# Message sums of a graph layer: half of the groups from rows split in two 12-bit parts, with a ring of 15 rows

## The chip, the cores and the metric

The kernel runs on one core of a Trainium2 chip. The metric is the device time of one execution in microseconds, the median of repeated runs. The engines are TensorE (PE, with its weight loads PEld), VectorE (DVE), ScalarE (ACT), GpSimd (POOL) and SyncE (SP). DMAs are issued from the queues of SyncE and ScalarE, and from POOL for gathers and scatters by index.

## The reference, cut to what matters

There are 6250 tokens of 256 values and 100000 edges sorted by target. The layer adds a graph convolution and a linear attention to its input, and then a mixture of 16 experts of which each token takes two.

```python
xn = _layernorm(x)
# graph convolution: the message sums are the second line
h = xn @ W
agg = segment_sum(norm[:, None] * h[src], dst)      # norm = dinv[src] * edge_weight * dinv[dst]
agg = agg + (dinv * dinv)[:, None] * h
# then + b, layer norm, mixing with xn, relu; attention over all tokens beside it
x = x + gcn + attention
# each token: two of 16 experts, (H=256 -> F=512 -> 256), weighted, layer norm
x = x + ffn(_layernorm(x))
```

## The kernel before, in words

The work of nearly every engine is put in order by hand. A loop counts slots; in each slot `c` from 0 to 781 POOL issues one gather of chunk `c` (128 edges), and all other steps are pieces that a `Weave` starts at given slots. An engine takes its instructions in the order in which they were emitted; POOL, SyncE and the others then run as fast as their waits allow.

Before the slots, the kernel turns the edges' targets, weights and sources into columns (`columns`: transposes on TensorE, copies on ScalarE), counts the degrees (`deg`), and writes the table `w_hs` to DRAM: the normalized rows of `x` times `dinv` (`table`, L522 and L524, staged in the big tile `Q`, stored by SyncE at L529).

In the slots, a chunk's message sum goes like this. At slot `c` POOL gathers 128 rows of 256 values from `w_hs` by the index column `src_t[:, c]` (L1306) into one of 12 rows of `rows3`, the ring `hrow`. VectorE builds a 128x128 matrix `hot` with the edge's weight where the target matches (L1310, a `tensor_scalar` of `iota_g` with two scalar columns). At slot `c + LAG`, LAG being 6, TensorE multiplies `hot` with the gathered rows in f32 (L1319; an f32 matmul is two instructions) into the group's accumulator. A group is 8 chunks. After its last chunk VectorE adds the accumulator, times `dinv`, into `agg` (L1331).

Woven in are: `attend` per token tile in the slots up to about 160 (keys, queries and the context; it writes its queries into `Q[:, t]` at L585), `own_term` (SyncE loads a tile of `w_hs`, ScalarE scales it, L648 and L650), the zero fills of `w_xslots` and `w_yslots` (L378, 1 MB each, on SyncE's queue), `residual` per pair of tiles from slot 171 on (transposes, products, layer norms: L688 to L756), `route` and `scatter` per phase of tiles (POOL writes tokens to slots of experts, L1005), `expert` per block of 128 slots (SyncE loads the weights, L1033; TensorE L1076, L1087 and L1098; ScalarE L1081 and L1094), and after the last chunk `combine` (POOL gathers the experts' rows, L1145). Memory that is free is handed on: `Places` gives tiles of `Q`, whose queries were read, to tokens, weights and results.

Of the kernel before, what the change touches and what calls it, by code (L numbers as in the profile page):

```python
# [22 lines left out]

F32 = mybir.dt.float32
BF = mybir.dt.bfloat16
I32 = mybir.dt.int32
# [86 lines left out]
NB3 = 2 * D  # L113
LAG = 6

# [17 lines left out]
def group_of(c):  # L133

    return (c + CPR // 2) // CPR


# [38 lines left out]
def gps_layer(ctx: ExitStack, tc: tile.TileContext, x, src, dst, ew, **rest):  # L176
# [6 lines left out]

    rows3 = top.tile([P, 3, EW], F32, name="rows3")
    loc_e, src_e, ew_e = rows3[:ER, 0, :], rows3[:ER, 1, :].bitcast(I32), rows3[:ER, 2, :]
    ident = top.tile([P, P], F32, name="ident")

    loc_t = top.tile([P, NCA], F32, name="loc_t")
    w_t = top.tile([P, NCA], F32, name="w_t")
    flag = top.tile([1, 1], I32, name="flag")  # L190
    with tc.tile_pool(name="chk", bufs=1) as cp, \
            tc.tile_pool(name="chk_ps", bufs=1, space=bass.MemoryType.PSUM) as cps, by_hand(tc):
        dst_e = cp.tile([ER, EW], I32, name="dst_e")
        v.memset(dst_e[:, PADC:], N - 1)
# [5 lines left out]
        for t0 in range(0, NFULL, 8):  # L200
# [25 lines left out]
        v.tensor_reduce(tot, n_out, axis=AX.X, op=OP.add)  # L226
        v.tensor_scalar(flag, tot, 0.0, None, op0=OP.is_equal)
    ok = nc.values_load(flag[0:1, 0:1], min_val=0, max_val=1,
                        skip_runtime_bounds_check_because="a comparison's result")
    with tc.If(ok) as cmp:  # L230
        windowed_layer(tc, X, rows3, ident, loc_t, w_t, **rest)
    with cmp.Else():
# [9 lines left out]
@with_exitstack  # L242
def windowed_layer(ctx: ExitStack, tc: tile.TileContext, X, rows3, ident, loc_t, w_t, W, b, gamma, beta, wqT, wkvT, wprojT, bproj,
                   gate_w, gate_b, experts, f_gamma, f_beta, out):
    nc = tc.nc
    v = nc.vector
    act = nc.scalar.activation
    src_e = rows3[:ER, 1, :].bitcast(I32)

# [6 lines left out]
    xslots = dram.tile([(MOST + 1) * P, D], F32, name="w_xslots")  # L256
    yslots = dram.tile([(MOST + 1) * P, D], F32, name="w_yslots")
    b2rows = dram.tile([NE * P, D], BF, name="w_b2rows")
    hand = ctx.enter_context(ExitStack())
    hand.enter_context(by_hand(tc))  # L260

    def one(shape, name, dt=F32):
        return keep.tile(shape, dt, name=name)


    iota_row = one([P, P], "iota_row")
    nc.gpsimd.iota(iota_row, pattern=[[1, P]], base=0, channel_multiplier=0,
                   allow_small_or_imprecise_dtypes=True)

    iota_g = one([P, 2, P], "iota_g")  # L270
    nc.gpsimd.iota(iota_g[:, 0, :], pattern=[[-P // 2, 2], [1, P // 2]], base=P // 2, channel_multiplier=0,
                   allow_small_or_imprecise_dtypes=True)
    nc.gpsimd.iota(iota_g[:, 1, :], pattern=[[1, P]], base=0, channel_multiplier=0,
                   allow_small_or_imprecise_dtypes=True)
# [27 lines left out]
    ones3 = one([3, P], "ones3", BF)  # L302
    src_t = one([P, NCA], "src_t", I32)

# [67 lines left out]

    def fill(a, first, end):

        zero = zero_b.bitcast(F32)
        for s in range(first, end, 8):
            q = min(8, end - s)
            nc.sync.dma_start(a[s * P:(s + q) * P, :].rearrange("(p q) c -> p q c", q=q),  # L378
                              zero[:, None, :].to_broadcast([P, q, D]))
            yield 8  # L380

    SOON = 88
    for _ in fill(xslots, 0, SOON):
        pass
    with tc.tile_pool(name="deg", bufs=1) as sp, \
# [59 lines left out]
        for n in (C // 2, C // 2, C, C, C):  # L445
            lo1 = sp.tile([P, 16, C], BF, name="lo1", bufs=2)
            for i in range(16):
                v.tensor_scalar(lo1[:, i, :n], lo_b[:, c0:c0 + n], float(i), None, op0=OP.is_equal)
            hw = sp.tile([P, HI, 3, C], BF, name="hw", bufs=2)
            for i in range(HI):  # L450
                for s in range(3):
                    v.scalar_tensor_tensor(hw[:, i, s, :n], hi_b[:, c0:c0 + n], float(i), w3[:, s, c0:c0 + n],
                                           op0=OP.is_equal, op1=OP.mult)
            for c in range(c0, min(c0 + n, NCH)):
                g0 = 4 * group_of(c)
                h0 = g0
                while h0 < g0 + HI:
                    i = h0 // HB
                    h1 = min(g0 + HI, (i + 1) * HB)
                    nc.tensor.matmul(deg[:, i, (h0 - i * HB) * 3:(h1 - i * HB) * 3], lo1[:, :, c - c0],  # L460
                                     hw[:, h0 - g0:h1 - g0, :, c - c0].rearrange("p h s -> p (h s)"),
                                     start=False, stop=False)
                    h0 = h1
            if c0 == 0:
                sf = sp.tile([ER, EW], F32, name="sf")
                nc.scalar.copy(sf, src_e)
                columns(nc, sps, ident, sf, src_t)
                two_sums()
            c0 += n
# [45 lines left out]

    Q = sums.tile([P, NT, D], F32, name="Q")
    TG = 7

    def table(t):
        r = rows(t)  # L520
        if t % 4 == 1:
            act(Q[:r, t, :], X[:r, t, :], AF.Identity, bias=nmr[:r, t:t + 1], scale=rsd[:r, t:t + 1])  # L522
        else:
            v.tensor_scalar(Q[:r, t, :], X[:r, t, :], mv1[:r, t, 0:1], rsd[:r, t:t + 1],  # L524
                            op0=OP.subtract, op1=OP.mult)
        if t % TG == TG - 1:
            t0 = t + 1 - TG
            n = min(NFULL, t0 + TG) - t0
            nc.sync.dma_start(hs[t0 * P:(t0 + n) * P, :].rearrange("(t p) c -> p t c", p=P), Q[:, t0:t0 + n, :])  # L529
            if n < TG:  # L530
                nc.sync.dma_start(hs[NFULL * P:, :], Q[:rows(NFULL), NFULL, :])

# [28 lines left out]
    def attend(t):  # L561
# [22 lines left out]
        v.scalar_tensor_tensor(kf[:r], e[:r, 0, :], 1.0, pos[:r, 0, :], op0=OP.min, op1=OP.add)  # L584
        v.scalar_tensor_tensor(Q[:r, t, :], e[:r, 1, :], 1.0, pos[:r, 1, :], op0=OP.min, op1=OP.add)  # L585
        yield 2
        if t == 0:
            kx.extend((bank("kx0"), bank("kx1")))
        for j in range(2):
            nc.tensor.matmul(kx[j][:, :D + 1], kf[:r, j * P:(j + 1) * P], xn[:r], start=(t == 0), stop=(t == NT - 1))  # L590

    def context():
# [47 lines left out]

    def queries(t0):

        return Q[:, t0:min(NT, t0 + 2), :]

    def own_term(t):

        r = rows(t)
        nc.sync.dma_start(agg(t)[:r], hs[t * P:t * P + r, :])  # L648
        yield 4
        nc.scalar.mul(agg(t)[:r], agg(t)[:r], dinv[:r, t:t + 1])  # L650
        begun.add(t)

    def residual(ts_):
# [30 lines left out]

        q = Q[:r0, t0:t1, :]
        q8 = q.rearrange("p t c -> p (t c)").rearrange("p (h d) -> p h d", d=HEAD)
# [518 lines left out]
    def spare(t, n=1):  # L1205
        return range(t, t + n), lambda: Q[:, t:t + n, :].rearrange("p t c -> p (t c)")

    hrow = rows3.rearrange("p a (i d) -> p (a i) d", d=D)
    NROW = 3 * EW // D
    homes = {"token": Places(*[spare(t) for t in range(4)]),  # L1210
# [6 lines left out]
                          spare(22, 6), spare(28, 6)),  # L1217
             "more": Places(*[((), lambda i=i: hrow[:, i, :]) for i in range(NROW)], *[spare(t) for t in range(9, 13)]),
             "got": Places(*[spare(t) for t in range(35, NT)])}

# [11 lines left out]
    for a, first in (yslots, 0), (xslots, SOON):  # L1232
        weave.add(fill_at, fill(a, first, MOST + 1))
        fill_at += 8 * ((MOST + 8 - first) // 8)
# [7 lines left out]
    for n, b in enumerate(PHASES):  # L1242
        flush = b == NT
        for t0 in range(a, b, 2):
            t1 = min(b, t0 + 2)
            at = max(at, min(NCH, 16 * t1 + 4) + LAG + 3)
            weave.add(at, residual(range(t0, t1)))
            last_at = at
            for t in range(t0, t1):
# [33 lines left out]
    weave.add(last_at + RES, load_last())  # L1283
    weave.add(last_at + RES + 22, shift(range(NT - NROW - 4, NT), last))
    at = last_at + RES
# [10 lines left out]
    weave.add(ready + 38, load_again())  # L1296
    hrows, hots, accs = {}, {}, {}
    done = []
    slot = -PRE
    while slot <= NCH + LAG or weave.steps:  # L1300
# [3 lines left out]
        if 0 <= c < NCH:  # L1304
            hrows[c] = hrow[:, c % NROW, :]
            nc.gpsimd.indirect_dma_start(  # L1306
                out=hrows[c], out_offset=None, in_=hs,
                in_offset=IndirectOffsetOnAxis(ap=src_t[:, c:c + 1], axis=0))
            hots[c] = mp.tile([P, P], F32, name="hot", bufs=LAG + 1)
            v.tensor_scalar(hots[c], iota_g[:, group_of(c) % 2, :], loc_t[:, c:c + 1], w_t[:, c:c + 1],  # L1310
                            op0=OP.is_equal, op1=OP.mult)
        c = slot - LAG
        if 0 <= c < NCH:
            g = group_of(c)
            begin = c == 0 or group_of(c - 1) != g
            end = c == NCH - 1 or group_of(c + 1) != g
            if begin:
                accs[g] = aps.tile([P, D], F32, name="acc")
            nc.tensor.matmul(accs[g], hots.pop(c), hrows.pop(c), start=begin, stop=end)  # L1319
            if end:  # L1320
# [12 lines left out]
        weave.run(slot)  # L1333
        slot += 1
    msg.close()
    hand.close()
# [521 lines left out]
```

## Time and profile before

| | |
|---|---|
| median of 15 runs | 1468.66 us (1463.33 to 1472.24) |
| profiled execution | 1466.18 us, span 1464.3 us |
| busy, PE / PEld / DVE / ACT / POOL | 1228.6 / 993.9 / 955.8 / 501.1 / 960.9 us |
| first gather to last gather (L1306) | 102.0 to 1205.2 us |
| granted TensorE clock, mean | 0.933 |

A group's line gives line, engine, operation, the tiles out<-in, the count, then the busy time and the mean of one in ns, then the idle time of the engine just before these instructions with what ended most of it. A wait's line gives the total in us, the times and the longest. In a table of stretches each engine has its busy time and its number of instructions in brackets. In a timeline the columns are start in us, duration in us, engine, line, operation, tiles, shapes, count, and in square brackets the engine's idle time before it. TensorE's busy time is modelled and overlaps weight loads, so a full TensorE is not one at its peak.

### The profile page before, as it was taken

To read this page: it belongs to the slowest core of one execution; us is meant where nothing else is said; L and a number is where in the kernel's file an instruction comes from. 1 tells how busy PE (TensorE), PEld (TensorE's weight loads), DVE (VectorE), ACT (ScalarE), POOL (GpSimd) and SP (SyncE) were. 2 spreads that over 40 slices of the span, in tenths; PEclk is the share of its full clock that TensorE was granted. 3 is DMA by queue.
4 is the path that set the end of the run, shared out by engine and by line. 5 is a ranking of instruction groups with operands and counts; after the bars stand their busy time and mean duration, and the time that the engine had idled before them with its cause. 6 is when DMAs were issued, how large, how long until landed. Compare 5 with 4: busy or idle time off the path is not lost. (4 is left out here: it accounts for less than half of the span.)

```text
span 1464.3 us, 24332 instructions
## 1 busy us (share of the span) xinstructions
PE 1228.6 (84%) x6923; PEld 993.9 (68%) x6923; DVE 955.8 (65%) x3302; ACT 501.1 (34%) x1354; POOL 960.9 (66%) x999
## 2 busy tenths in 40 slices
PE   4879999978777788989879799788988997968880
PEld 3836666656665677868768687677877886857660
DVE  7954454458887484756847568375684666568885
ACT  2764444422222122313223122232332333434451
POOL 1017777777767777777777777777777773167643
PEclk9999999999877899999999899998999998989995
DMA  8989933333335678768778687776768886989993
GB/s 260 314 293 374 381 108 102 106 103 115 102 105 165 222 237 279 263 231 269 273 233 290 202 270 264 264 269 226 263 219 278 293 292 220 310 293 387 379 316 96
DMA packets 176921, 353.83 MB, mean 242 GB/s; under 512 B 26769, under 2 KB 116020, under 8 KB 176770
## 3 DMA queue, kind: packets, MB, share of 16 engines
q1 hardware_dynamic: 128790, 223.10, 43.9%
q0 software_dynamic: 47712, 128.17, 27.5%
q8 instruction: 61, 1.00, 0.3%
q10 hardware_dynamic: 268, 0.82, 0.2%
q14 instruction: 90, 0.74, 0.2%
HBM read 277.60 MB, written 74.38 MB: 240 GB/s over the span
## 5 line engine op out<-in xcount | busy, mean ns | idle before, releaser
L1306 POOL DMA_INDIRECT rows<-w_hs,src_t x782 | 756.3, 967 | 327.2 <-issue 96.6
L1319 PE MATMUL acc<-rows,hot 128*128 128x256 f32 x1564 | 448.8, 403 | 90.9 <-DMA rows<-w_hs,src_t 76.8
L1310 DVE TENSOR_SCALAR hot<-iota_g,loc_t,w_t 128x128 f32<-128x128 f32 x782 | 270.9, 363 | 282.2 <-PE acc L1319 275.5
L1319 PEld LDWEIGHTS acc<-rows,hot 128*128 128x128 f32 x1564 | 279.9, 199 | 168.8 <-issue 73.0
L1005 POOL DMA_INDIRECT w_xslots<-Q,slot_i x98 | 99.1, 1011 | 78.2 <-ACT Q L1081 39.6
L1098 PE MATMUL yp<-early,hT 128*128 128x256 f32 x592 | 147.8, 395 | 1.2 <-ACT hT L1094 1.1
L1145 POOL DMA_INDIRECT Q<-w_yslots,slot_i x98 | 99.6, 1016 | 68.0 <-DVE xn L1161 22.2
L1087 PE MATMUL hp<-Q,early 128*128 128x128 f32 x992 | 127.7, 285 | 9.9 <-ACT Q L1081 9.9
L1087 PEld LDWEIGHTS hp<-Q,early 128*128 128x128 f32 x992 | 124.9, 200 | 14.7 <-ACT Q L1081 12.0
L1094 ACT ACTIVATE hT<-hp,early 128x128 f32<-128x128 f32 x296 | 84.3, 368 | 143.7 <-PE hp L1087 107.0
L1098 PEld LDWEIGHTS yp<-early,hT 128*128 128x128 f32 x592 | 116.5, 200 | 18.8 <-ACT hT L1094 2.4
L1081 ACT COPY Q<-xtp 128x256 f32<-128x256 f32 x114 | 42.2, 370 | 224.0 <-PE xtp L1076 221.9
L1087 PE MATMUL hp<-Q 128*128 128x128 f32 x832 | 106.8, 284 | 7.9 <-ACT Q L1081 7.9
L1087 PEld LDWEIGHTS hp<-Q 128*128 128x128 f32 x832 | 103.8, 199 | 12.5 <-ACT Q L1081 10.6
L576 PE MATMUL kq<-early,xnT 128*128 128x512 f32 (+1 forms) x196 | 95.8, 613 | 3.6 <-ACT xnT L572 3.6
L324 ACT ACTIVATE sd<-mv,eps_t 128x2 f32<-128x2 f32 (+2 forms) x76 | 22.6, 298 | 216.3 <-DVE mv L320 210.7
L1098 PE MATMUL yp<-Q,hT 128*128 128x256 f32 x320 | 78.2, 389 | 1.6 <-ACT hT L1094 1.5
L706 PE MATMUL hp<-w_sb,two_a 128*128 128x256 f32 (+1 forms) x196 | 58.2, 449 | 19.4 <-ACT two_a L678 19.4
L1098 PEld LDWEIGHTS yp<-Q,hT 128*128 128x128 f32 x320 | 60.1, 194 | 11.3 <-ACT hT L1094 3.9
L1331 DVE SCALAR_TENSOR_TENSOR agg<-acc,dinv,agg 64x256 f32<-64x256 f32 x135 | 64.9, 481 | 2.8
L706 PEld LDWEIGHTS hp<-w_sb,two_a 128*128 128x128 f32 (+1 forms) x196 | 42.6, 225 | 30.4 <-ACT two_a L678 21.9
L1108 DVE TENSOR_TENSOR Q<-yp,early 128x256 f32<-128x256 f32 x61 | 25.7, 422 | 55.8 <-PE yp L1098 55.7
(306 smaller groups left out, 1741.2 us busy)
## 6 DMA issues: line engine op xcount, KB each, us to landing
early<-in_experts SPq DMA_DIRECT2D x61, 642.0 KB
early<-in_experts SPq DMA_DIRECT2D x62, 512.0 KB
Q<-in_experts SPq DMA_DIRECT2D x52, 512.0 KB
Q<-in_experts SPq DMA_DIRECT2D x27, 642.0 KB
w_xslots<-zero_b SPq DMA_DIRECT2D x16, 1024.0 KB
w_yslots<-zero_b SPq DMA_DIRECT2D x16, 1024.0 KB
Q<-w_xslots SPq DMA_DIRECT2D x114, 128.0 KB
w_yslots<-Q SPq DMA_DIRECT2D x114, 128.0 KB
```

The lines of the kernel that those rows point to most:

```text
L576: nc.tensor.matmul(kq[:r], xnT[:, k, :r], wkq[:, k, :], start=(k == 0), stop=(k == 1))
L706: nc.tensor.matmul(hp[:r0, i, :], agT[:, k, i * P:i * P + r0], w_sb[:, k, :], start=(k == 0), stop=(k == 1))
L1005: i = nc.gpsimd.indirect_dma_start(out=xslots, out_offset=IndirectOffsetOnAxis(ap=slot_i[:r, t, k:k + 1], axis=0), in_=y[:r], in_offset=No ...
L1081: nc.scalar.copy(xT, tp[:, :2, :])
L1087: nc.tensor.matmul(hp[:, f, :], w1[:, c, f * P:(f + 1) * P], xT[:, c, :], start=(c == 0), stop=(c == 1))
L1094: act(hT[:, f, :], hp[:, f, :], AF.Relu, bias=b1[:, f:f + 1], scale=1.0)
L1098: nc.tensor.matmul(yp[:, :D], hT[:, f, :], w2[:, f, :], start=(f == 0), stop=(f == FJ - 1 and not as_row))
L1145: g = nc.gpsimd.indirect_dma_start(out=got[i, k]()[:r], out_offset=None, in_=yslots, in_offset=IndirectOffsetOnAxis(ap=slot_i[:r, t, k:k + ...
L1306: nc.gpsimd.indirect_dma_start(out=hrows[c], out_offset=None, in_=hs, in_offset=IndirectOffsetOnAxis(ap=src_t[:, c:c + 1], axis=0))
L1310: v.tensor_scalar(hots[c], iota_g[:, group_of(c) % 2, :], loc_t[:, c:c + 1], w_t[:, c:c + 1], op0=OP.is_equal, op1=OP.mult)
L1319: nc.tensor.matmul(accs[g], hots.pop(c), hrows.pop(c), start=begin, stop=end)
L1331: v.scalar_tensor_tensor(agg(t)[p0:p1], acc[p0:p1, :], dinv[p0:p1, t:t + 1], agg(t)[p0:p1], op0=OP.mult, op1=OP.add)
```

## The change

For the groups below 24, and from 40 on for those with an odd number, a chunk is summed in another way. `hot` is then a plain 0/1 matrix in the type float32r, built for two chunks at once by a `tensor_tensor` comparison of `iota_g` with `loc_t`. The gathered row is multiplied by the edge's weight and split into two parts: ScalarE writes `high`, the product in float32r, and VectorE writes `low`, the exact product minus `high`. TensorE multiplies `hot` with `high` and with `low`. The other groups are summed as before, their `hot` matrices allocated in pairs.

The gathered rows get a ring of 15, `high` and `low` rings of 5 each. To make room, `rows3` and the conversion of the sources into columns move to the first pool (before the check of the edges decides the branch), `Q` shrinks from 49 to 36 tiles, the tiles of `w_hs` from 35 on are staged in places 7 to 20, the queries of tiles from 36 on are stored to a new DRAM tensor `w_q` and loaded again 8 slots before their `residual`, and what lay in the ring's and `Q`'s last tiles late in the kernel (`more`, `got`) moves to a pool `late` that is opened after the ring is closed. The later zero fills go from SyncE's queue to ScalarE's. LAG becomes 7 (6 for chunks not in parts), and the residuals start one slot later with it.

```diff
-LAG = 6
+LAG = 7
+SPLIT = 3
+QT = 36
+RING_ROWS, RING_PARTS = 15, 5
+def in_parts(g):
+    return g < 24 or (g >= 40 and g % 2 == 1)
...
+        sf = cp.tile([ER, EW], F32, name="sf")
+        nc.scalar.copy(sf, src_e)
+        columns(nc, cps, ident, sf, src_t)
...
-    def fill(a, first, end):
+    def fill(eng, a, first, end):
...
-            nc.sync.dma_start(a[s * P:(s + q) * P, :].rearrange("(p q) c -> p q c", q=q),
+            eng.dma_start(a[s * P:(s + q) * P, :].rearrange("(p q) c -> p q c", q=q),
...
-    Q = sums.tile([P, NT, D], F32, name="Q")
+    Q = sums.tile([P, QT, D], F32, name="Q")
+    staged = [t if t < 5 * TG else t - 4 * TG for t in range(NT)]
...
+        if t >= QT:
+            nc.sync.dma_start(w_q[(t - QT) * P:(t - QT) * P + r, :], q[:r])
...
+    def load_queries(ts_):
+        for i, t in enumerate(ts_):
+            r = rows(t)
+            nc.sync.dma_start(queries(ts_[0])[:r, i, :], w_q[(t - QT) * P:(t - QT) * P + r, :])
...
-        weave.add(fill_at, fill(a, first, MOST + 1))
+        weave.add(fill_at, fill(nc.scalar, a, first, MOST + 1))
...
+            if t0 >= QT:
+                weave.add(at - 8, load_queries(range(t0, t1)))
...
-            hrows[c] = hrow[:, c % NROW, :]
+            hrows[c] = rp.tile([P, D], F32, name="hrow", bufs=RING_ROWS)
...
-            hots[c] = mp.tile([P, P], F32, name="hot", bufs=LAG + 1)
-            v.tensor_scalar(hots[c], iota_g[:, group_of(c) % 2, :], loc_t[:, c:c + 1], w_t[:, c:c + 1],
-                            op0=OP.is_equal, op1=OP.mult)
-        c = slot - LAG
-        if 0 <= c < NCH:
+        c = slot - 3
+        if 0 <= c < NCH and c % 2 == 0:
+            full = [P, 2, P]
+            g = group_of(c)
+            if in_parts(g):
+                hot = mp.tile(full, FR, name="hot", bufs=4)
+                v.tensor_tensor(hot, iota_g[:, g % 2:g % 2 + 1, :].to_broadcast(full),
+                                loc_t[:, c:c + 2, None].to_broadcast(full), op=OP.is_equal)
+            else:
+                hot = mp.tile(full, F32, name="hot", bufs=4)
+                for i in range(2):
+                    v.tensor_scalar(hot[:, i, :], iota_g[:, g % 2, :], loc_t[:, c + i:c + i + 1], w_t[:, c + i:c + i + 1],
+                                    op0=OP.is_equal, op1=OP.mult)
+            hots[c], hots[c + 1] = hot[:, 0, :], hot[:, 1, :]
+        c = slot - SPLIT
+        if 0 <= c < NCH and in_parts(group_of(c)):
+            highs[c] = rp.tile([P, D], FR, name="high", bufs=RING_PARTS)
+            act(highs[c], hrows[c], AF.Identity, scale=w_t[:, c:c + 1])
+        c = slot - SPLIT - 1
+        if 0 <= c < NCH and in_parts(group_of(c)):
+            lows[c] = rp.tile([P, D], FR, name="low", bufs=RING_PARTS)
+            v.scalar_tensor_tensor(lows[c], hrows.pop(c), w_t[:, c:c + 1], highs[c].bitcast(F32), op0=OP.mult, op1=OP.subtract)
+        for c, parts in ((slot - LAG, True), (slot - LAG + 1, False)):
+            if not (0 <= c < NCH and in_parts(group_of(c)) == parts):
+                continue
...
+            if parts:
+                nc.tensor.matmul(accs[g], hot, highs.pop(c), start=begin, stop=False)
+                nc.tensor.matmul(accs[g], hot, lows.pop(c), start=False, stop=end)
+            else:
+                nc.tensor.matmul(accs[g], hot, hrows.pop(c), start=begin, stop=end)
...
+        if slot == NCH + LAG + 1:
+            ringed.close()
```

## The prediction

> **What bounds the kernel now.** I read the page first. TensorE is its busiest engine, but the chain of waits holds only the last 9 us, so a bound has to be found stage by stage. Next came the table by stretches, on the message stage.
>
> ```profile
> core 0: us, PE busy (x) PEld busy (x) DVE busy (x) ACT busy (x) POOL busy (x), PEclk, DMA share, GB/s
> 180.00:240.00 60.00, 60.00 (x239) 42.18 (x238) 29.70 (x86) 28.42 (x59) 45.68 (x48) 1.00 0.40 120
> 360.00:420.00 60.00, 45.75 (x202) 35.76 (x200) 51.61 (x164) 14.34 (x31) 42.03 (x43) 0.84 0.34 98
> 1140.00:1200.00 60.00, 58.76 (x352) 51.90 (x352) 34.16 (x99) 18.77 (x55) 45.60 (x48) 1.00 0.88 300
> ```
>
> TensorE's load swings; POOL starts 48 DMAs in nearly every 60 us, one per 1.25 us. So I took POOL's own groups, cut to 102 to 1206 us:
>
> ```profile
> L1306 POOL DMA_INDIRECT rows<-w_hs,src_t x782 | 756.3, 967 | 327.2 <-issue 96.6 <-DMA w_yslots<-zero_b 83.7 <-PE acc L1319 59.7
> L1005 POOL DMA_INDIRECT w_xslots<-Q,slot_i x80 | 79.9, 999 | 24.4 <-issue 14.3 <-DMA w_xslots<-Q,slot_i 6.7 <-DMA rows<-w_hs,src_t 1.2
> ```
>
> Leave out the 83.7 us before the first gather: 756.3 + (327.2 - 83.7) + 79.9 + 24.4 = 1104.1 us, the whole 1104 us stage. Is any of that idle time a real wait?
>
> ```profile
> POOL rows L1306 <- issue: 96.6, 317, 0.3
> POOL rows L1306 <- PE acc L1319: 59.7, 179, 4.2
> L1306 POOL DMA_INDIRECT rows<-w_hs,src_t x782: 942/946/1525, 102.0 to 1205.2; - x196
> ```
>
> Where nothing releases a gather, the gap before it is 96.6/317 = 0.305 us, so that is POOL's own overhead. The 179 gaps put down to TensorE cost 59.7 - 179 x 0.305 = 5.1 us beyond it, those of L1087 another 0.5. So 5.6 us of the stage waits for anybody. **POOL's gathers bound 102 to 1206 us**, at 0.946 + 0.305 = 1.251 us each; TensorE only keeps up. The other thing to explain is the gathers' spread: median 946 ns, mean 967, longest 1525. The timeline shows what stands beside the long ones:
>
> ```profile
> 186.40 0.41 DVE L584 SCALAR_TENSOR_TENSOR row<-two_a,two_b 128x256 f32<-128x256 f32 x1
> 186.56 1.07 POOL L1306 DMA_INDIRECT rows<-w_hs,src_t  x1 [0.30 <-issue]
> 186.73 0.42 DVE L585 SCALAR_TENSOR_TENSOR Q<-two_a,two_b 128x256 f32<-128x256 f32 x1
> ...
> 315.03 1.50 POOL L1306 DMA_INDIRECT rows<-w_hs,src_t  x1 [0.30 <-PE acc L1319]
> 315.04 0.68 DVE L688 TENSOR_TENSOR qk<-Q,ksum 128x512 f32<-128x512 f32 x1
> ...
> 858.82 0.69 DVE L712 TENSOR_TENSOR h<-hp,bias_b 128x512 f32<-128x512 f32 x1 [1.38 <-PE hp L706]
> 858.92 0.95 POOL L1306 DMA_INDIRECT rows<-w_hs,src_t  x1 [0.30 <-PE hp L706]
> ```
>
> L584 and L688 read two SBUF tensors. A gather beginning under one ends 0.82 us after it: 186.81 to 187.63, 315.72 to 316.53. An undisturbed gather takes 0.946, so it is held if the operation still runs 0.126 us after its start. L585, begun 0.17 us after a start, lengthens nothing and is itself not slowed. L712, with one operand in PSUM, holds nothing.
>
> **The change, part by part.** Slots pace the program: one gather each, so POOL's cost counts in full and the others' only past 1.25 us a slot. Chunks in parts: groups below 24 hold chunks 0 to 187, odd groups 41 to 97 hold 29 x 8 = 232; together 420.
>
> *VectorE.* Removed: 420 one-hots at L1310 (363 ns, one tensor input). Added: per two chunks a comparison of shape 128x256, two SBUF inputs (nearest row L1130, 407 ns), and per chunk a `low` of 128x256, two SBUF inputs and a scalar column (L1161, 482 ns). In the 180 row VectorE carries 29.70/48 = 0.62 us a slot; it becomes 0.62 - 0.36 + 0.20 + 0.48 = 0.94. That fits in 1.25, so its time costs nothing; without that cover 0.32 x 420 = 134 us would be at stake.
>
> *What these inputs do to POOL.* This is the term that counts. An operation of length d beginning at random against a period of 1.25 us holds the next gather for (d - 0.126)^2 / (2 x 1.25) on average: `low` 0.356^2/2.5 = 0.051, comparison 0.281^2/2.5 = 0.032 per pair or 0.016 per chunk. L1310 held nothing (one input). Sum 0.067 x 420 = 28 us. Bounds: 0 if every `low` falls behind a gather's start; 0.356 x 420 = 150 us if each begins just before one. `low` follows `high`, which follows a landing, and landings and ScalarE's queue vary, so random phase is nearest; but a delayed gather moves away from the next `low`, so I take 22.
>
> The Trainium skill's page "SBUF — State Buffer", section "Who interferes with whom", states the contention between a two-SBUF-input VectorE instruction and a GpSimd instruction that reads SBUF, but as a lock for the whole instruction: whichever starts first blocks the other. By that rule a `low` begun under a gather would also wait for its end, 0.47 us on average in three quarters of the cases, VectorE would reach 1.3 us a slot in the first stretch, and some 10 us would be added. The L585 row above speaks against that half, and the sum leaves it out.
>
> *ScalarE.* Added: 420 `high` scalings, 128x256 with one scale column (L650, 509 ns; with two columns L566, 602), and the 23 later fills, which SyncE issues now (L378: 654 ns shortest, 2771 median). First 188 slots: 28.42/48 = 0.59, + 0.51, + 23 x 0.654/188 = 0.08, is 1.18 a slot; it fits by 0.07. Upper ends: 0.59 + 0.60 + 0.34 = 1.53. I take the lower end: the median fill was issued into saturated queues (in the table of stretches 120 to 180 us shows a DMA share of 1.06), while spread over 188 slots they bring 1 MB per 10 us. Queued behind a `high` that waits for its gather are the attend steps, for which TensorE waits, and on VectorE behind `low` the sums into `agg` and the attend steps again; in the later groups, at 18.77/48 + 0.25 = 0.65 a slot, nothing is tight.
>
> *TensorE.* Two f32 matmul instructions per chunk go, 403 ns each; two single ones of the new type come. No row has the type. Consecutive f32 instructions of 256 columns begin 0.217 us apart (four at L1319 in 1.03 us), 10 bf16 ones of 512 columns at L477 take 2.33 us, 0.105 per 256. So a chunk goes from 0.43 to between 0.21 and 4 x 0.217 = 0.87 us: from -0.22 to +0.44. I take -0.22, since operands cut to 12 bits are nearest to bf16. Off the path it is worth nothing: POOL waits 5.6 us for others.
>
> *Ring and lag.* 15 rows instead of 12, released by `low` four slots after the gather or by TensorE after six: the 5.6 us of waits go, I take -4. Residuals begin one slot later, so does the end: +1.3. The rings of 5 parts let `high` run one slot behind TensorE: nothing while both have room.
>
> *Queues and start.* The fills leave SyncE; the 13 query stores and 13 loads join it. A load waits for a residual two pairs earlier, 32 slots back, and expert loads queue behind it: nothing. The staged tiles that are written twice wait for a store that was issued some 8 us earlier (L529's seven stores begin over 13.7 us): nothing. The table's last stores no longer share queues with two fills (-2 at best), while the moved conversion of `src` (L466 1.0, L153 1.6 us) may hold up the weights' region (+3 at worst): 0. The `late` rows are needed after 1206 us: 0.
>
> **Sum.** +22 - 4 + 1.3 = +19.3 us, none of it in the tail after 1206 us, whose engines carry the same work. The profiled execution took 1466.2 us (span 1464.3): 1485.5. The median of the runs shown, 1468.66, lies 2.5 above that one: 1488.
>
> **Rivals.**
> *Parts cost nothing and the ring's waits go* (faster): by the packets of the gathers' queue between 220 and 400 us a gather has landed 2.4 us after its start; `high` 0.5 and two hand-overs of some 0.2 let `low` run from 3.3 to 3.78, before the third next gather reads at 3.75 + 0.13. If ScalarE is always prompt, no gather is held: -5.6 - 2 + 1.3 gives 1462. It decides if `low` is late by less than 0.1 us; attend steps of 0.6 us in ScalarE's queue speak against it. Halfway (4 us of holding) nothing moves: 1468.
> *ScalarE becomes the bound in the first 188 slots*: with fills at the median 1.44 us a slot, with both upper ends 1.53: 188 x 0.19 to 0.28 = 36 to 53, and 16 of holding in the later 232 chunks: 1517 to 1536.
> *The new type doesn't run in one pass*: TensorE, full in the 180 row at 1.25 a slot, gets 0.44 more: 188 x 0.44 = 83 us, later covered in part: 1550 or more. The Trainium skill's "FP8 and Floating Point Precision", section "TensorE Precision Notes", counts four passes for true FP32 and tells of a reduced mode that reads 4 bytes and truncates; by it a chunk would take two passes instead of four, the lower end.
>
> **Chances.** Forecast 0.62 (lock 10 to 35 us: 1476 to 1502); faster 0.12; nothing moves 0.07; ScalarE 0.13; TensorE 0.06. A measurement here tells 0.2%, 2.9 us, from no change. Faster 0.12, same 0.07, slower 0.81. The range takes in the forecast, no change and most of ScalarE's case: 1465 to 1520.
>
> **What would show it.** Right: the gathers' mean rises from 967 to about 995 ns (22 us over 782) with the minimum at 942, and to about 1020 where all chunks are in parts, while groups 24 to 39 stay; gaps stay 0.305; TensorE's busy time falls. Wrong: the mean stays near 967 (the faster rival); POOL's gaps grow behind ScalarE or `high` (second) or behind matmuls (third); or the time after the last gather moves by more than 2 us, of which nothing here speaks.

## The result and the profile after

The changed kernel takes 1509.0 us (median of 9 runs, 1504.85 to 1516.7) against 1467.8 us of the kernel before beside it (46 runs): a ratio of 1.0279, 95% interval 1.0262 to 1.0297, 41 us slower. The profiled execution took 1502.9 us (span 1501.2), some 6 us below its median; against the profiled 1466.2 us of before that is 36.8 us, and this is what the traces can account for. The forecast was 1488, a change of 20 us: the sign and the main mechanism were right, the size was half of what came.

The table by stretches first (same columns as before).

```profile
core 0: us, PE busy (x) PEld busy (x) DVE busy (x) ACT busy (x) POOL busy (x), PEclk, DMA share, GB/s
180.00:240.00 60.00, 48.79 (x205) 32.08 (x203) 38.97 (x98) 40.59 (x94) 46.29 (x46) 0.94 0.60 188
360.00:420.00 60.00, 47.41 (x223) 36.42 (x221) 50.22 (x149) 17.43 (x39) 40.17 (x43) 0.89 0.35 102
```

In the first stretch TensorE's busy time went from 60 to 49 us, VectorE's rose from 30 to 39, ScalarE's from 28 to 41, all below 60; and POOL got 46 DMAs through instead of 48. So POOL still sets the pace, and it is slower. POOL's groups, cut to the gather stage (101 to 1243 us), then its waits there and the gathers' line:

```profile
L1338 POOL DMA_INDIRECT hrow<-w_hs,src_t x782 | 784.4, 1003 | 333.1 <-issue 97.1 <-DMA hT<-w_hs 84.2 <-PE acc L1376 24.9
L1025 POOL DMA_INDIRECT w_xslots<-Q,slot_i x80 | 82.0, 1025 | 24.4 <-issue 15.2 <-DMA w_xslots<-Q,slot_i 6.7 <-DVE mv L329 1.2
```
```profile
POOL hrow L1338 <- issue: 97.1, 314, 1.7
POOL hrow L1338 <- PE acc L1376: 24.9, 52, 3.8
```
```profile
L1338 POOL DMA_INDIRECT hrow<-w_hs,src_t x782: 942/946/2673, 103.7 to 1242.4; - x196
```

The 782 gathers are busy 784.4 us instead of 756.3 (mean 1003 ns instead of 967) with the same minimum and median; the longest now takes 2673 ns. The free gap stayed at 97.1/314 = 0.309 us (0.305 without the one of 1.7). From TensorE there are fewer waits, but 24.9 - 52 x 0.305 = 9.0 us of them lie beyond the free gap (5.1 before). The first gather starts at 103.7 instead of 102.0. The account of the two profiled executions:

| term | before | after | difference |
|---|---|---|---|
| first gather starts | 102.0 | 103.7 | +1.7 |
| gathers busy | 756.3 | 784.4 | +28.1 |
| scatters busy (80 in the stage) | 79.9 | 82.0 | +2.1 |
| all POOL gaps beyond 0.305 us | 5.4 | 10.6 | +5.2 |
| from the last gather's start to the end | 259.1 | 258.7 | -0.4 |

The sum, 36.7, is the whole difference. Now the gathers alone (line L1338), cut at chunks 188 and 316; the chunks between them are groups 24 to 39, of which none is in parts:

```profile
103.55:352.62 249.07, 191.77 (x188) 0.92 0.63 198
352.62:557.91 205.29, 124.86 (x128) 0.85 0.50 159
557.91:1243.55 685.64, 467.76 (x466) 0.93 0.75 252
```

191.77/188 is 1020 ns a gather where all chunks are in parts (975 before), 124.86/128 is 975 where none is (982 before), 467.76/466 is 1004 after that (960 before). And in that last stretch it is not the odd groups' own gathers that grew (964 to 971 ns by their records) but those of the even groups, 956 to 1036: in these groups most `low`s (155 of 232) start when POOL is five or more gathers further on, and 150 when it is at a later group.

What holds them is seen in the timeline:

```profile
182.98 0.41 DVE L1347 TENSOR_TENSOR hot<-iota_g,loc_t 128x256 fp32r<-128x256 f32 x1
183.31 0.86 DVE L1362 SCALAR_TENSOR_TENSOR low<-hrow,w_t,high 128x256 fp32r<-128x256 f32 x2
183.45 1.89 POOL L1338 DMA_INDIRECT hrow<-w_hs,src_t  x1 [0.30 <-DVE hot L1347]
184.11 0.41 DVE L1347 TENSOR_TENSOR hot<-iota_g,loc_t 128x256 fp32r<-128x256 f32 x1
...
610.46 1.72 POOL L1338 DMA_INDIRECT hrow<-w_hs,src_t  x1 [0.30 <-issue]
610.69 0.67 DVE L751 SCALAR_TENSOR_TENSOR X<-h,X 128x512 f32<-128x512 f32 x1
```

The gather that starts at 183.45, under the first of two `low`s, isn't released between them, nor between them and the comparison that follows without a pause: it ends at 185.34, 0.82 us after that comparison's end (184.52). That is not the rule, though. Another such pair, with a gather that starts as far into it (0.14 us), lets the gather go 0.82 us after the first one's end:

```profile
634.37 0.87 DVE L1362 SCALAR_TENSOR_TENSOR low<-hrow,w_t,high 128x256 fp32r<-128x256 f32 x2
634.51 1.16 POOL L1338 DMA_INDIRECT hrow<-w_hs,src_t  x1 [0.30 <-PE yp L1118]
```

Of 135 gathers held by an operation that another one followed without a pause, 116 ended 0.82 us after the first operation's end and 19 later; what decides between the two isn't known.

Now each gather's and scatter's time beyond its undisturbed one (946 and 973 ns) is put to the VectorE operation that runs some 0.06 us after its start. The total of 48.8 us (18.6 before) contains 20.9 of `low` (94 of the 152 that met one were over 30 ns longer), 7.0 of the comparisons (29 of 46) and 4.6 of six gathers like the one at 610.46, where L751 stands directly behind a sum into `agg`. Cut in another way, 36.3 us (13.4 before) lie up to 0.82 us after the end of the operation that was running when the gather started (0.85 for scatters; this takes in all that is lengthened by 30 ns or less), and 12.5 us (5.3 before) beyond that, under operations that began after the gather.

### The profile page after: what moved, and what is told of

Its sections match the earlier page's. It is cut to its first block, busy times and chain, and to the rows that moved or that the text cites. A ratio compares the mean times of both kernels' runs of the same rounds, so it can differ in the third digit from the quotient of the medians.

```text
span 1501.2 us, 25295 instructions
## 1 busy us (share of the span) xinstructions
PE 1204.4 (80%) x6923; PEld 974.7 (65%) x6923; DVE 1061.5 (71%) x3512; ACT 670.2 (45%) x1774; POOL 990.9 (66%) x998
## 5 line engine op out<-in xcount | busy, mean ns | idle before, releaser
L1338 POOL DMA_INDIRECT hrow<-w_hs,src_t x782 | 784.4, 1003 | 333.1 <-issue 97.1
L1362 DVE SCALAR_TENSOR_TENSOR low<-hrow,w_t,high 128x256 fp32r<-128x256 f32 x420 | 199.1, 479 | 138.3 <-ACT high L1358 133.1
L1358 ACT ACTIVATE high<-hrow,w_t 128x256 fp32r<-128x256 f32 x420 | 203.7, 506 | 208.3 <-DMA hrow<-w_hs,src_t 142.3
L1376 PE MATMUL acc<-hrow,hot 128*128 128x256 f32 x724 | 214.0, 410 | 37.6 <-DMA hrow<-w_hs,src_t 24.2
L1376 PEld LDWEIGHTS acc<-hrow,hot 128*128 128x128 f32 x724 | 128.6, 201 | 64.3 <-DVE hot L1352 21.0
L1373 PE MATMUL acc<-high,hot 128*128 128x256 f32 x420 | 159.8, 395 | 5.6 <-ACT high L1358 5.5
L1374 PE MATMUL acc<-low,hot 128*128 128x256 f32 x420 | 124.4, 309 | 35.3 <-DVE low L1362 33.9
L1165 POOL DMA_INDIRECT late<-w_yslots,slot_i x98 | 99.4, 1014 | 66.9 <-DVE xn L1181 20.9
L584 PE MATMUL kq<-early,xnT 128*128 128x512 f32 (+1 forms) x196 | 103.3, 652 | 39.5 <-ACT xnT L580 39.2
L1107 PEld LDWEIGHTS hp<-Q 128*128 128x128 f32 x832 | 104.4, 203 | 18.7 <-ACT Q L1101 17.9
L1352 DVE TENSOR_SCALAR hot<-iota_g,loc_t,w_t 128x128 f32<-128x128 f32 x362 | 108.3, 358 | 0.0
L1373 PEld LDWEIGHTS acc<-high,hot 128*128 128x128 f32 x420 | 86.4, 206 | 19.8 <-issue 10.9
```

The source lines that it names most:

```text
L584: nc.tensor.matmul(kq[:r], xnT[:, k, :r], wkq[:, k, :], start=(k == 0), stop=(k == 1))
L1107: nc.tensor.matmul(hp[:, f, :], w1[:, c, f * P:(f + 1) * P], xT[:, c, :], start=(c == 0), stop=(c == 1))
L1165: g = nc.gpsimd.indirect_dma_start(out=got[i, k]()[:r], out_offset=None, in_=yslots, in_offset=IndirectOffsetOnAxis(ap=slot_i[:r, t, k:k + ...
L1338: nc.gpsimd.indirect_dma_start(out=hrows[c], out_offset=None, in_=hs, in_offset=IndirectOffsetOnAxis(ap=src_t[:, c:c + 1], axis=0))
L1352: v.tensor_scalar(hot[:, i, :], iota_g[:, g % 2, :], loc_t[:, c + i:c + i + 1], w_t[:, c + i:c + i + 1], op0=OP.is_equal, op1=OP.mult)
L1358: act(highs[c], hrows[c], AF.Identity, scale=w_t[:, c:c + 1])
```

## The experiments

All kernels are variants of the changed one. "Waits" are POOL's gaps between the first and the last gather beyond 0.305 us each; "tail" runs from the last gather's start to the end; both, with the gathers and the first gather's start, are from each kernel's one profiled execution. The ratio is to the kernel before on the same chip, where its medians are 1467.8 to 1469.6 us.

| kernel | median us | ratio, 95% interval | first gather | gathers busy, mean ns | waits | tail |
|---|---|---|---|---|---|---|
| before | 1468.7 | | 102.0 | 756.3, 967 | 5.4 | 259.1 |
| changed | 1509.0 | 1.0279 [1.0262, 1.0297] | 103.7 | 784.4, 1003 | 10.6 | 258.7 |
| no_parts | 1478.6 | 1.0081 [1.0055, 1.0107] | 105.2 | 765.6, 979 | 4.1 | 259.8 |
| one_by_one | 1474.2 | 1.0052 [1.0033, 1.0072] | 106.3 | 762.3, 975 | 2.0 | 257.9 |
| extra_two | 1504.1 | 1.0252 [1.0217, 1.0287] | 106.9 | 781.7, 1000 | 5.2 | 262.1 |
| extra_one | 1490.7 | 1.0144 [1.0120, 1.0168] | 108.8 | 769.3, 984 | 4.8 | 261.4 |
| extra_psum_3 | 1485.4 | 1.0118 [1.0089, 1.0147] | 104.6 | 759.5, 971 | 10.0 | 263.7 |
| low_single | 1496.0 | 1.0199 [1.0166, 1.0233] | 105.2 | 769.6, 984 | 10.5 | 265.9 |
| hot_scalar | 1510.7 | 1.0284 [1.0253, 1.0315] | 104.4 | 783.0, 1001 | 12.9 | 262.8 |
| both_single | 1493.9 | 1.0179 [1.0155, 1.0203] | 106.8 | 763.8, 977 | 9.7 | 266.1 |
| until_20 | 1502.5 | 1.0237 [1.0214, 1.0261] | 105.3 | 778.8, 996 | 2.0 | 262.4 |
| late_only_3 | 1492.3 | 1.0182 [1.0145, 1.0218] | 105.0 | 769.7, 984 | 6.9 | 262.6 |

**What is left without the parts.** `no_parts`:

```diff
-    return g < 24 or (g >= 40 and g % 2 == 1)
+    return False
```

Expected: 

> No chunk goes in parts; the 15-row ring, the moved fills, the moved conversion of src, the smaller staging tile and the one-hots made in pairs all stay. Theory (two-input VectorE operations hold the gathers): the 30 us of holding and the 5 us of new waits in groups 24 to 39 go, the later start of 1.7 us may stay: 1467 to 1471, gather mean 967 ns. Rival (the ring, the moved queues or the paired one-hots cost the time): 1485 or more, with the gather mean at 967 all the same.

It came 8 to 12 us above the theory's 1467 to 1471 and below the rival's 1485. So the parts make some 30 of the 41 us, and something else costs 9. The gathers' mean is not 967 but 979, and the timeline shows an operation that the prediction had cleared:

```profile
137.80 0.59 DVE L1352 TENSOR_SCALAR hot<-iota_g,loc_t,w_t 128x128 f32<-128x128 f32 x2
138.13 2.01 POOL L1338 DMA_INDIRECT hrow<-w_hs,src_t  x1 [0.30 <-PE tp L552]
138.31 0.42 DVE L592 SCALAR_TENSOR_TENSOR row<-two_a,two_b 128x256 f32<-128x256 f32 x1
138.98 0.59 DVE L1352 TENSOR_SCALAR hot<-iota_g,loc_t,w_t 128x128 f32<-128x128 f32 x2
```

The one-hot has one tensor input, yet the gather that starts under a pair of them is held, through the attend steps and into the next pair: 9.2 us in all are held under L1352, where the kernel before had 2.0 under L1310. `one_by_one` makes them one a slot again:

```diff
-        if 0 <= c < NCH and c % 2 == 0:
-            ...
-                for i in range(2):
-                    v.tensor_scalar(hot[:, i, :], ...)
+        if 0 <= c < NCH:
+            v.tensor_scalar(hots[c], iota_g[:, group_of(c) % 2, :], loc_t[:, c:c + 1], w_t[:, c:c + 1],
+                            op0=OP.is_equal, op1=OP.mult)
```

Expected: 

> As no_parts (no chunk in parts), but each slot makes its own one-hot with one VectorE instruction, as the kernel before does, instead of two every second slot. Holding theory, with back-to-back runs as a part of it: the one-hots' holding (9.2 us in no_parts, 2.0 us in the kernel before) falls by 7 us, and about 3 us stay for the later first gather: 1470 to 1473, gather mean 979 falls to about 969 ns. Rival (the rest of the change, ring and queues, costs the 9 us): still 1477 to 1480.

1474.2, just above the theory's 1470 to 1473: 4.4 us go, not 7, and the intervals of the two ratios overlap (7.3 us are still held under the one-hots, which now run three slots later than in the kernel before). What stays above the kernel before, 0.5%, is in the profiled executions 6.0 us of gathers and 4.3 us of a later first gather, against 3.4 us fewer waits, with the ring of 15 rows.

**One operation alone.** On top of `one_by_one`, 420 VectorE operations were added that nobody reads, one for each chunk that the change takes in parts, and nothing on ScalarE or TensorE. The three differ in their operands:

```diff
+            extra = rp.tile([P, D], F32, name="extra", bufs=2)
+            v.scalar_tensor_tensor(extra, hrows[c], w_t[:, c:c + 1], hrows[c], op0=OP.mult, op1=OP.subtract)   # extra_two
+            v.tensor_scalar(extra, hrows[c], w_t[:, c:c + 1], w_t[:, c:c + 1], op0=OP.mult, op1=OP.subtract)   # extra_one
+            v.scalar_tensor_tensor(extra, hrows[c], w_t[:, c:c + 1], nothing, op0=OP.mult, op1=OP.subtract)    # extra_psum_3: nothing is in PSUM
```

Expected: 

> As one_by_one, plus one VectorE operation for each of the 420 chunks that the change would take in parts: row times weight minus row, 128x256, two SBUF inputs, into a tile that nobody reads; no high or low part, no new type, no work on ScalarE or TensorE. Holding theory: 13 us (each alone: a gather is held if it starts 0.08 to 0.36 us after the operation's start, so 0.28^2/2.5 = 0.030 us each) to 28 us (with its share in back-to-back runs), on top of one_by_one: 1484 to 1500. Rival (ScalarE's and TensorE's parts cost the time, not this operation): no more than 2 us on top of one_by_one.

Expected: 

> As extra_two, but the operation has one tensor input and the weight column twice: row times weight minus weight. Holding theory: the window is 0.15 to 0.28 us after its start, 0.13^2/2.5 = 0.007 us each, 3 us, up to 9 with runs: 3 to 9 us above one_by_one, and at least 10 under extra_two. Rival (VectorE's load or order delays others): within 3 us of extra_two, since the operation is nearly as long.

Expected: 

> As extra_two (one_by_one plus 420 operations of 128x256 that nobody reads), but the subtracted operand lies in PSUM, a tile of zeros, so that one tensor input is left in SBUF; the pool of the other PSUM tiles has 5 banks instead of 6 for it. Holding theory: an operation with a PSUM operand holds no gather by itself, so what is left is what it adds to runs: 1 to 6 us above one_by_one, 1.004 to 1.010 of the kernel before. Rival (the VectorE time of the operation or its wait for the row costs the 30 us of extra_two): 1.020 to 1.027.

`extra_two` costs 30 us over `one_by_one`, as much as the whole splitting in parts. That is 2 us past the end of its holding price, and 4 past the 1500 stated; in the profiled executions 19.4 us are gathers, 4.8 scatters. `extra_one` costs 16.5, more than the 3 to 9 expected, of which 7.0 are gathers, but it lies 13.5 under `extra_two`. With the operand in PSUM the gathers are as in `one_by_one` (759.5 and 762.3 us busy); the time is still 11 us above it, in waits (+8.0) and tail (+5.8). Its ratio of 1.0118 lies above the 1.004 to 1.010 expected and below the rival's 1.020. Whether the missing PSUM bank or VectorE's load makes these waits was not separated; `extra_two`, with the same load and all banks, has 5.2 us of them, but its gathers are held, which may give TensorE time. The same start of a gather, 0.19 us into the operation, first in `extra_two`, then in `extra_psum_3`:

```profile
158.52 0.48 DVE L1357 SCALAR_TENSOR_TENSOR extra<-hrow,w_t 128x256 f32<-128x256 f32 x1 [2.38 <-DMA hrow<-w_hs,src_t]
158.71 1.11 POOL L1338 DMA_INDIRECT hrow<-w_hs,src_t  x1 [0.30 <-DMA hrow<-w_hs,src_t]
```
```profile
151.86 0.47 DVE L1360 SCALAR_TENSOR_TENSOR extra<-hrow,w_t,nothing 128x256 f32<-128x256 f32 x1
152.05 0.94 POOL L1341 DMA_INDIRECT hrow<-w_hs,src_t  x1 [0.30 <-DVE hot L1347]
```

The first gather ends 0.82 us after the operation (159.00 to 159.82), the second takes its plain 0.94. Counted over all gathers that start 0.145 to 0.27 us after such an operation's start, and held by over 30 ns: 45 of 45 for `low` in the changed kernel, 42 of 42 in `extra_two`, 35 of 40 in `extra_one`, 4 of 56 in `extra_psum_3` (two for 37 and 38 ns, two for 0.7 and 0.8 us by operations with two SBUF inputs queued behind it). Under `low` the window opens some 0.08 us after the start (of 27 starts between 0.08 and 0.145, 26 were held), with one tensor and a scalar column at about 0.145; under the comparison L1347 it opens earlier (15 of 16 starts between 0.02 and 0.08 were held). So the mechanism is shown: at the same length on VectorE (medians 477 and 473 ns) and in the same order, the place of the operand decides whether a gather is held.

**The pieces of the changed kernel.** `low_single` and `hot_scalar` take the second SBUF tensor from one operation each, `both_single` from both. `low_single` and `both_single` leave out the true subtraction, so their sums differ.

```diff
-            v.scalar_tensor_tensor(lows[c], hrows.pop(c), w_t[:, c:c + 1], highs[c].bitcast(F32), op0=OP.mult, op1=OP.subtract)
+            v.tensor_scalar(lows[c], hrows.pop(c), w_t[:, c:c + 1], highs[c][:, 0:1].bitcast(F32), op0=OP.mult, op1=OP.subtract)   # low_single
-                v.tensor_tensor(hot, iota_g[:, g % 2:g % 2 + 1, :].to_broadcast(full), ...)
+                for i in range(2):                                                                                                # hot_scalar
+                    v.tensor_scalar(hot[:, i, :], iota_g[:, g % 2, :], loc_t[:, c + i:c + i + 1], None, op0=OP.is_equal)
```

Expected: 

> The low part is made from the row, its weight and one column of the high part as two scalars, so that it has one tensor input in SBUF instead of two but still waits for the high part; the true subtraction is left out. Holding theory: 20.9 us of holding by the low parts go: about 1488, gather mean 1003 falls to about 976 ns. Rival (the queueing behind ScalarE's high part, or TensorE's parts): the same order and the same waits, so no change, 1505 to 1510. Rival (VectorE's load): only what a shorter operation saves, under 8 us.

Expected: 

> The comparison of two chunks with two SBUF inputs (407 ns) is replaced by two comparisons with one tensor input and a scalar column each (some 360 ns each); nothing else changes. Holding theory: the 43 gathers that it held (7.0 us) are free, minus a little for a busier VectorE: 1500 to 1504. Rival (VectorE's load is what costs): 0.16 us more work for each of 420 chunks, 1515 or more. Gather mean in groups below 24: 1020 ns falls to about 1003 by the theory.

Expected: 

> Both edits: the low part with one tensor input (its true subtraction left out) and the comparisons with one tensor input each. Holding theory: 28 us go, 1479 to 1483, gather mean about 968 ns, and what is left above the kernel before is new waits in groups 16 to 39 and the later start. Rival (queueing or TensorE): 1505 or more, or slower for VectorE's longer comparisons.

`low_single` gains 13 us, not 21. What is held under `low` falls from 20.9 to 8.4 us, not to nothing, because an operation with one tensor and two scalar columns holds too; and the tail is 7 us longer, with other values going to the experts (not traced further). From the first to the last gather it gains 1138.7 - 1123.4 = 15.3. `hot_scalar` was a miss: 7 us expected, none came (+1.7, within the spread). Its comparisons hold 2.2 us instead of 7.0, but `low` holds 26.8 instead of 20.9. The comparisons stand directly before a `low`, so a gather let off by the one may be caught by the other; this was not traced gather by gather. `both_single` gains 15 (1138.7 - 1116.9 = 21.8 in the gather stage, against 28 expected), and its holding is 27.9 instead of 48.8 us. None of the three moved the new waits (9.7 to 12.9).

**The new waits.** `until_20` ends the early parts 32 chunks sooner:

```diff
-    return g < 24 or (g >= 40 and g % 2 == 1)
+    return g < 20 or (g >= 40 and g % 2 == 1)
```

Expected: 

> As the changed kernel, but groups 20 to 23 (chunks 156 to 187) are not in parts, so that parts end before the first residual steps at slot 171. Theory (VectorE cannot carry both in slots 171 to 191, and falls behind): the waits of 10.4 us in chunks 188 to 315 fall to about 5, and 32 fewer chunks hold 2 us less: 1501 to 1503 against 1509. Rival (the new waits in groups 24 to 39 come from the longer lag or TensorE's order): only the 2 us go, 1506 to 1508, and the waits stay at 10.

1502.5, as expected, with the waits between chunks 188 and 316 down from 10.4 to 2.2 us. In that stretch, changed kernel first:

```profile
POOL hrow L1338 <- PE acc L1376: 20.4, 37, 3.8
```
```profile
POOL hrow L1338 <- PE acc L1376: 11.0, 29, 1.5
```

The four kernels with parts up to chunk 187 (changed, `low_single`, `hot_scalar`, `both_single`) have 10.0 to 13.0 us of waits there; before, `no_parts`, `late_only_3` and `until_20` have 2.2 to 6.9. So in the changed kernel they come with the overlap of the last early parts and the first residuals (slot 171 on). What in it makes them stays open. VectorE is busy 12.77 of the 15 us from 320 to 335 (7.88 in `until_20`), and the granted TensorE clock there is also lower (0.73 against 0.80). VectorE's load alone is a weak reason: before has 13.93 of 15 us from 335 to 350, and `extra_two`, with an operation as long as `low` for the same chunks, has 5.3 us of waits in that stretch. `extra_psum_3`, without any parts, has 10.1.

**Early or late groups.** `late_only_3`:

```diff
-    return g < 24 or (g >= 40 and g % 2 == 1)
+    return g >= 40 and g % 2 == 1
```

Expected: 

> As the changed kernel, but only the odd groups from 41 on (232 chunks) go in parts; the first 24 groups as in no_parts. By the rows of no_parts and of the changed kernel: 15 us more holding of the gathers in the even groups (where the low parts run), 2 us elsewhere, no new waits in chunks 188 to 315, on top of no_parts' 9 us: 1.017 to 1.020 of the kernel before. If the time came from the early groups alone: 1.007.

1.0182, as expected: the late groups make 1.0 of the 2.0 points between `no_parts` and the changed kernel (15 us), the early ones with their waits, by subtraction, the other half. `early_only_2` (only groups below 24) was to close the sum, and `best_2` to keep what is useful of the change: `one_by_one` with the one-hots in the slot of their gather, and the conversion of `src` on GpSimd and VectorE.

Expected: 

> As the changed kernel, but only groups below 24 (chunks 0 to 187) go in parts; the later ones all as in no_parts. By the rows of no_parts and of the changed kernel: 5 us more holding in chunks 0 to 187 and 6 us more waits in chunks 188 to 315, on top of no_parts' 9 us: 1.013 to 1.016 of the kernel before.

Expected: 

> What of the change is left without its costs: no chunk in parts, one one-hot per slot in the slot of its gather as in the kernel before, the ring of 15 rows and the other moves, and the conversion of src moved on to GpSimd (copy) and VectorE (out of PSUM), so that it no longer stands on ScalarE ahead of the first branch. By the ledger: 3 us fewer waits, start later by 0.5 us: 0.997 to 1.000 of the kernel before. If the ring's rows and the moved queues cost something that the traces don't show: 1.002 or more.

These two ran only on chips where every kernel, the one before too (1717.5 and 1735.7 us), took some 250 us longer, with 234 to 321 us of waits between the gathers. There `early_only_2` stands at 1.0205 [1.0172, 1.0238] and `best_2` at 1.0100 [1.0069, 1.0131] of the kernel before; with another bound on that stage neither settles its question, and no version was found that beats the kernel before. Other runs on those chips tell no more: the same two kernels at 1.0218 and 1.0124, that of `late_only_3` at 1.0415 and 1.0452, that of `extra_psum_3` at 1.0199 and 1.0205.

**The start.** The conversion of the sources, moved into the first pool, in the changed kernel, and then the first memset after the branch in the kernel before:

```profile
11.63 1.06 ACT L239 CAST sf<-rows 98x1024 f32<-98x1024 int32 x1
13.70 1.57 ACT L162 CAST src_t<-tpe 128x392 int32<-128x392 f32 x2 [1.01 <-PE tpe L161]
14.50 0.27 DVE L293 MEMSET zero_b<- 128x256 uint32 x1 [3.07 <-DMA X<-in_x]
```
```profile
13.11 0.27 DVE L283 MEMSET zero_b<- 128x256 uint32 x1 [0.91 <-ACT w_t L153]
```

`flag` is ready 0.8 us earlier than before, yet the branch's first work starts 1.4 us later, while ScalarE is still writing `src_t`. In the ten variants of the table the first gather starts at 104.4 to 108.8. In `best_2`, with the conversion on other engines, that memset came at 16.3, later still: VectorE, which then copies `src_t`, takes the branch after it. So the later start after the branch is seen in the traces, but no run takes it away; how much of the 1.7 to 6.8 us is spread between executions stays open, since the kernel before has one profile.

## Why the prediction was right or wrong

- **POOL's gathers bound the stage, and VectorE's operands decide:** right. The gathers' time with its minimum unchanged, the free gap, groups 24 to 39 as before and 1020 ns where all chunks are in parts came as written; `extra_two` and `extra_psum_3` show the cause.
- **The lock term, +22:** mis-sized, and the first of the two steps that failed. Gathers and scatters grew by 30.2 us (28.1 + 2.1). Of these, 22.9 (36.3 - 13.4) come from the operation that was running when the gather started, which is what the term priced, and 7.2 (12.5 - 5.3) from operations that began after it, which the prediction put at nothing ("L585, begun 0.17 us after a start, lengthens nothing"). One of its own rows showed such a case and was read as a gather beginning under L688. The gather began at 315.03, 0.01 us before L688, in the end of a one-hot, and L688 held it all the same:

```profile
314.77 0.33 DVE L1310 TENSOR_SCALAR hot<-iota_g,loc_t,w_t 128x128 f32<-128x128 f32 x1
```

  That 22.9 is so near to 22 is in part luck: the formula opens the window at the operation's start, while for `low` it opens some 0.08 us later, and with a random phase 0.276^2/2.5 = 0.030 us each makes 13 us for the `low`s, not 21. They held 15.7 us in this way, so the phase was not quite random, or the window isn't quite that.
- **"L1310 held nothing (one input)":** too strong. It held 2.0 us; in pairs the same operation held 9.2 (`no_parts`). The Trainium skill's "SBUF — State Buffer", section "Who interferes with whom", lists `tensor_scalar` among the operations that can enter a two-port mode and then contend; `extra_one`'s 35 of 40 agree. The same section lets whichever starts first block the other for the whole instruction. Half of that holds here: 45 of 45 gathers that started 0.145 to 0.27 us into a `low` waited for its end. The other half isn't seen: the longest of the 420 `low`s took 552 ns, median 479, so none was stretched to a gather's 946.
- **Ring and waits, -4:** wrong in sign, +5.2, the second step that failed and the larger one (9.2 us). With the ring and without parts the waits did shrink, by 3.4 (`one_by_one`). What the sum lacked is a term for waits that the parts bring: "that fits in 1.25, so its time costs nothing" was read from the 180 to 240 us row, which has no residuals. Where parts and residuals meet (slots 171 to 187) new waits came; `until_20` takes 8 of the 10.4 us between chunks 188 and 316 away. Through which engine's queue they come stays open.
- **Start, 0:** +1.7 in the profiled execution. Of the two bounds given, the trace shows the side of the moved conversion (+3 at worst): the first work after the branch is 1.4 us later.
- **LAG, +1.3:** the time after the last gather went from 259.1 to 258.7. Tails range from 257.9 to 266.1 over these kernels, so 1.3 can't be read from one execution.
- The four steps, +8.2, +9.2, +1.7 and -1.7, make the 17.4 between the sum of 19.3 and the 36.7 measured. The other 3.5 us to the median are the profiled execution of the changed kernel, which lies 6 below its median where that of before lay 2.5 below.
- **The rivals:** the parts are not free. ScalarE did not become the bound: `high` takes 506 ns as costed, the 180 row shows 40.59 of 60 us. The new type is no slower:

```profile
L1358 ACT ACTIVATE high<-hrow,w_t 128x256 fp32r<-128x256 f32 x420 | 203.7, 506 | 208.3 <-DMA hrow<-w_hs,src_t 142.3
L1373 PE MATMUL acc<-high,hot 128*128 128x256 f32 x420 | 159.8, 395 | 5.6 <-ACT high L1358 5.5
L1374 PE MATMUL acc<-low,hot 128*128 128x256 f32 x420 | 124.4, 309 | 35.3 <-DVE low L1362 33.9
```

A chunk takes 395 + 309 ns by these means instead of two of 410 (L1376), and TensorE's busy time fell from 1228.6 to 1204.4 us: less work on an engine that bounded nothing.

## What to carry to other kernels

Where GpSimd's gathers set the pace, price a VectorE operation by its operands and by its neighbours: two SBUF tensors hold a gather to the operation's end, one SBUF tensor with scalar columns holds it later and less, a PSUM operand hardly ever (4 of 56), and operations that follow each other without a pause sometimes hold as one long one (19 of 135). Check that added work fits in the stretch where the most other work stands, not in a typical one. And measure such an operation by adding it alone: `extra_two` told in one run what the parts cost (30 of the 41 us).

## What the runs showed of the hardware that was not expected

- A run of VectorE operations can hold one gather through all of them: the longest gather of the changed kernel took 2673 ns instead of 946 (start 779.01, at the end of a `low`; behind it a comparison, two more `low`s and L708, which ends at 780.86, 0.82 us before the gather does). Most gathers are let go at the first operation's end.
- An operation with two SBUF inputs queued directly behind another can hold a gather that started up to 0.23 us before it (L751 behind L1388, which has an operand in PSUM, 610.69 after 610.46: 1.72 us; six such gathers). It doesn't always: L585 in the kernel before stood as directly behind L584 and let the gather at 186.56 end 0.82 us after L584.
- One tensor in SBUF is enough for a `tensor_scalar` to hold a gather (35 of 40), but only from about 0.145 us after its start, so short one-hots hold little: the 363 ns one of the kernel before held 21 of the 67 gathers that started 0.145 to 0.27 us into it.
